# The int8 feed-forward part taken by halves of 512 rows, with its down products regrouped

## The chip, the cores and the metric

The kernel runs on one core of one Trainium2 chip. The metric is the device time of one execution in microseconds (us); the kernel before has a median of 733.33 us over three runs (732.94 to 734.95). TensorE (PE) multiplies, VectorE (DVE), ScalarE (ACT) and GpSimd (POOL) work on rows of 128 partitions, SyncE (SP) and ScalarE start the transfers (DMA) that matter here. The program gives each engine its instructions in one fixed order.

## The reference, cut to what matters

Two transformer layers over a (4, 256, 256) input. The last part is a feed-forward layer with int8 weights, added to its input and layer-normed. As called here, `x` has 1,024 rows of 256; the hidden width is 1,024.

```python
def _qmatmul(x, w_int8, scale):
    y = jnp.einsum('bsh,ho->bso', x, w_int8.astype(x.dtype))
    return y * scale
gate = silu(_qmatmul(x, w_gate, s_gate))
up = _qmatmul(x, w_up, s_up)
x = _layernorm(x + _qmatmul(gate * up, w_down, s_down))
```

What comes ahead of it (rotary attention with 16 heads, a feed-forward layer with a Hadamard transform, an mLSTM block with its own feed-forward layer) takes the first 675 us and is computed in the same way in both kernels.

## The kernel before, in words

The int8 values are kept as `F32R`, a 32-bit type whose products the trace shows as one matmul record each; an activation is split into a high part in that type and the rest (`rest`, L856), so every product is the sum of two. The part works batch by batch, 256 rows each:

- `ffn2_in` (L868) transposes a batch's rows (four 128x128 transposes, L876, into one PSUM bank), takes the high part with a ScalarE copy (L878) and the low part with a DVE subtraction (L857): tile `qx`.
- `ffn2_up` (L882) makes, for each of `NH` = 8 blocks of 128 hidden columns, the gate and the up product side by side in one PSUM bank, 256 columns each: four matmuls each, two chunks of the contraction times high and low part (`mm_parts`, L861). Then come SiLU on ScalarE (L890), scaling and product on DVE (L891), the high part on ScalarE (L894), the low part on DVE for odd blocks and on GpSimd for even ones (L857): tile `qh`.
- `ffn2_sums` (L901) makes the down products: for each of a batch's two tiles of 128 rows, 16 matmuls of 256 columns (L909) into a bank `po`. DVE scales them, adds the input and takes mean and variance (L914, L915, L502, L503).
- `ffn2_down` (L918) computes the inverse root on DVE alone, by a bit trick and three Newton steps (`rsqrt`, L50 to L63: 13 small instructions), normalizes on DVE (L924) and writes the batch out. The last batch, `ffn2_end` (L932), takes the root from ScalarE (L939) and one Newton step on DVE instead, normalizes one row tile on each engine and writes by two queues. ScalarE loads the table for the root (L898) at the end of the last up block.

The banks come from two cycles: `bank("d")` hands out `mm` and `sc` in turn, `bank("m")` `pt` and `ot`; each name has two buffers, so four banks are in turn on either side. The order is written by hand at the end: up products of batch 0, with those of batch 2 begun in between, then batch 1 and 3; a batch's down products stand some blocks after its last up block. A scheduler then orders the instructions of each engine by this.

Just ahead stands the second half's `ffn1` (rows 512 to 1,023 of the layer before): 32 fp32 down products (L561), and a layernorm of its last rows on DVE with the same 13-instruction root (L53 to L63, L512), which gives `xb[1]`.

Of the kernel before, what the change touches and what calls it, by code (L numbers as in the profile page):

```python
# [24 lines left out]
NH = FF // P  # L25
HALF = NT // 2
NJH = HALF // P
# [3 lines left out]
LN_EPS = 1e-5  # L31
# [7 lines left out]
def tile_two_layers(ctx: ExitStack, tc: tile.TileContext, a: dict, out: bass.AP):  # L39
    nc = tc.nc  # L40

    const = ctx.enter_context(tc.tile_pool(name="const", bufs=1))
    small = ctx.enter_context(tc.tile_pool(name="small", bufs=3))
    psum = ctx.enter_context(tc.tile_pool(name="psum", bufs=2, space=bass.MemoryType.PSUM))

    def bank(tag):
        return psum.tile([P, 512], F32, tag=tag, name=f"ps_{tag}")


    def rsqrt(v, n, scale, eps):  # L50

        ve = small.tile([P, n], F32, tag="rs_v", name="rs_v")
        nc.vector.tensor_scalar(ve, v, scale, eps, ALU.mult, ALU.add)  # L53
        sh = small.tile([P, n], I32, tag="rs_sh", name="rs_sh")
        nc.vector.tensor_single_scalar(sh, ve.bitcast(I32), 1, ALU.logical_shift_right)
        y = small.tile([P, n], F32, tag="rs_y", name="rs_y")
        nc.vector.tensor_scalar(y.bitcast(I32), sh, -1.0, RSQRT_MAGIC, ALU.mult, ALU.add)
        nc.vector.tensor_scalar_mul(ve, ve, -0.5)
        t = small.tile([P, n], F32, tag="rs_t", name="rs_t")
        for _ in range(3):  # L60
            nc.vector.tensor_tensor(t, y, y, ALU.mult)
            nc.vector.tensor_tensor(t, t, ve, ALU.mult)
            nc.vector.scalar_tensor_tensor(y, t, 1.5, y, ALU.add, ALU.mult)  # L63
        return y
# [14 lines left out]
    ps = bank("pt")  # L79
# [45 lines left out]
    ident = cst[:, 896:1024]  # L125
# [276 lines left out]
    ps = {}  # L402
    prs = {}
    rest = []
    for bb in range(2):
# [3 lines left out]
        po = bank("ot")  # L409
# [29 lines left out]
    rest = []  # L439
    for bb in range(2):  # L440
        po = bank("ot")
# [9 lines left out]
    work = ctx.enter_context(tc.tile_pool(name="work", bufs=2))  # L451
# [38 lines left out]
    xb = [work.tile([P, NJH, D], F32, tag=f"xb{n}", name=f"xb{n}", bufs=1) for n in halves]  # L490
    xs = [work.tile([P, NJH, D], F32, tag=f"xs{n}", name=f"xs{n}", bufs=1) for n in halves]
# [112 lines left out]
    bias = mix.tile([2 * 32, 2], F32, tag="bias", name="bias")  # L604
# [251 lines left out]
    def rest(engine, v, hi, lo):  # L856
        engine.tensor_tensor(lo, v, hi.bitcast(F32), ALU.subtract)  # L857
# [5 lines left out]
    out_v = out.rearrange("b (t p) d -> p b t d", p=P)  # L863

    def rows_of(t, b):
        return t[b // 2][:, 2 * (b % 2) : 2 * (b % 2) + 2, :]

    def ffn2_in(b):  # L868

        xd = rows_of(xb, b)  # L870
        x = work.tile([P, 2, KC, S], F32R, tag="fm", name="qx")
        pt = bank("d")
        for c in range(KC):
            for j in range(2):
                at = c * S + j * P
                nc.tensor.transpose(pt[:, at : at + P], xd[:, j, c * P : (c + 1) * P], ident)  # L876
        by_c = pt.rearrange("p (c s) -> p c s", c=KC)
        nc.scalar.copy(x[:, 0], by_c)  # L878
        rest(nc.vector, by_c, x[:, 0], x[:, 1])
        return x  # L880

    def ffn2_up(x, hT, last=False):  # L882
        for c in range(NH):
            cols = slice(c * P, (c + 1) * P)
            ps = bank("d")
            pg, pu = ps[:, 0:S], ps[:, S:]
            for dst, w in ((pg, q_gate), (pu, q_up)):
                mm_parts(dst, [(w[:, i, cols], x[:, k, i, :]) for i in range(KC) for k in range(2)])
            g = split.tile([P, S], F32, tag="gq", name="gq", bufs=4)
            nc.scalar.activation(g, pg, AF.Silu, scale=s_gu[:, c : c + 1])  # L890
            nc.vector.scalar_tensor_tensor(  # L891
                g, pu, s_gu[:, NH + c : NH + c + 1], g, ALU.mult, ALU.mult
            )
            copied = nc.scalar.copy(hT[:, 0, c, :], g)  # L894
            rest(nc.vector if c % 2 else nc.gpsimd, g, hT[:, 0, c, :], hT[:, 1, c, :])
            if last and c == NH - 1:
                with tc.issue_after(copied.ins):
                    nc.scalar.activation(small.tile([P, 1], F32, tag="junk1", name="junk1"), eps, AF.Sqrt)  # L898
            yield 0.9

    def ffn2_sums(b, hT, mv):  # L901


        xd, xe = rows_of(xb, b), rows_of(xs, b)
        po = [bank("m")[:, :D] for _ in range(2)]
        for j, blocks in ((0, range(0, NH - 1)), (1, range(0, NH // 2)), (0, (NH - 1,)), (1, range(NH // 2, NH))):
            for i in blocks:
                for k in range(2):
                    nc.tensor.matmul(  # L909
                        po[j], lhsT=hT[:, k, i, j * P : (j + 1) * P], rhs=q_down[:, i, :],  # L910
                        start=(i == 0 and k == 0), stop=(i == NH - 1 and k == 1),
                    )
        for j in range(2):
            nc.vector.tensor_tensor(xe[:, j, :], po[j], s_down, ALU.mult)  # L914
            nc.vector.tensor_tensor(xe[:, j, :], xe[:, j, :], xd[:, j, :], ALU.add)  # L915
            statistics(xe[:, j, :], mv[:, j, :])

    def ffn2_down(b, hT):  # L918
        xe = rows_of(xs, b)
        mv = small.tile([P, 2, 2], F32, tag="out_mv", name="out_mv")  # L920
        ffn2_sums(b, hT, mv)
        rstd = rsqrt(mv[:, :, 1], 2, 1.0, LN_EPS)
        for j in range(2):
            nc.vector.tensor_scalar(  # L924
                xe[:, j, :], xe[:, j, :], mv[:, j, 0:1], rstd[:, j : j + 1], ALU.subtract, ALU.mult
            )
        nc.sync.dma_start(out_v[:, b], xe)

    eps = late.tile([P, 1], F32, tag="eps", name="eps")
    nc.gpsimd.memset(eps, LN_EPS)  # L930

    def ffn2_end(b, hT):  # L932


        xe = rows_of(xs, b)
        mv = small.tile([P, 2, 2], F32, tag="out_mv", name="out_mv")
        ffn2_sums(b, hT, mv)
        root = small.tile([P, 2], F32, tag="rs_v", name="root")
        nc.scalar.activation(root, mv[:, :, 1], AF.Sqrt, bias=eps)  # L939
        ve = small.tile([P, 2], F32, tag="rs_sh", name="ve")  # L940
        nc.vector.tensor_scalar(ve, mv[:, :, 1], LN_EPS, -0.5, ALU.add, ALU.mult)
        rstd = small.tile([P, 2], F32, tag="rs_y", name="rstd")
        nc.vector.reciprocal(rstd, root)
        t = small.tile([P, 2], F32, tag="rs_t", name="rs_t")
        nc.vector.tensor_tensor(t, rstd, rstd, ALU.mult)
        nc.vector.tensor_tensor(t, t, ve, ALU.mult)
        nc.vector.scalar_tensor_tensor(rstd, t, 1.5, rstd, ALU.add, ALU.mult)
        shift = small.tile([P, 1], F32, tag="shift", name="shift")
        nc.vector.scalar_tensor_tensor(shift, mv[:, 0, 0:1], -1.0, rstd[:, 0:1], ALU.mult, ALU.mult)
        nc.vector.tensor_scalar(  # L950
            xe[:, 1, :], xe[:, 1, :], mv[:, 1, 0:1], rstd[:, 1:2], ALU.subtract, ALU.mult
        )
        nc.sync.dma_start(out_v[:, b, 1:2], xe[:, 1:2])
        nc.scalar.activation(xe[:, 0, :], xe[:, 0, :], AF.Identity, bias=shift, scale=rstd[:, 0:1])
        nc.scalar.dma_start(out_v[:, b, 0:1], xe[:, 0:1])


    def merge(first, other):
# [26 lines left out]
    one = ffn1(0, "d")  # L985
# [4 lines left out]
    left = one  # L990
    merge(mlstm(1), left)
    mix.release()
    split = tc.alloc_tile_pool(name="split", bufs=3, side="right")
    qh = [split.tile([P, 2, NH, S], F32R, tag="qh", name=f"qh{b}") for b in range(3)]
    one = ffn1(1, "m")
    merge(chain(take(1, one), [6.0]), left)
    run(left)
    run(one)
    ups, hts = {}, qh

    def begin(b):
        ups[b] = ffn2_up(ffn2_in(b), hts[b], b == B - 1)

    begin(0)
    run(take(5, ups[0]))
    begin(2)
    run(ups[0])
    run(take(2, ups[2]))
    begin(1)
    run(take(2, ups[2]))  # L1010
    ffn2_down(0, hts[0])
    run(ups[2])
    hts.append(split.tile([P, 2, NH, S], F32R, tag="qh", name="qh3"))
    begin(3)
    run(take(4, ups[1]))
    ffn2_down(2, hts[2])
    run(ups[1])
    run(take(4, ups[3]))
    ffn2_down(1, hts[1])
    run(ups[3])  # L1020
    ffn2_end(3, hts[3])
    split.release()
    hid.release()
    wts.release()


# [93 lines left out]
```

## Time and profile before

| what | before |
|---|---|
| median of 3 runs | 733.33 us (732.94 to 734.95) |
| the profiled execution | 733.4 us, of which its span on the core is 731.6 us |
| PE busy | 719.2 us, 98% of the span |
| DVE, ACT, POOL busy | 406.8, 242.2, 179.6 us |
| first int8 up product | 675.71 us |
| last batch's down products begin | 720.09 us |
| last transfer is issued | 728.57 us |
| granted TensorE clock | 0.998 of full |

The profile comes from one execution. Times in the trace are counted from the span's start. A matmul's duration in the trace includes its way through the array, and neighbours overlap; what a matmul costs in a stream is therefore the distance from one start to the next. An fp32 product stands in the trace as two matmul records.

### The profile page before, as it was taken

Reading aid. Unit: us, or ns where it says so; the run is one execution under the profiler, and the core shown is the slowest. Engines: PE = TensorE matmul, PEld = TensorE weight load, DVE = VectorE, ACT = ScalarE, POOL = GpSimd, SP = SyncE. Lnnn points to the kernel's source line nnn. Section 1 sums busy time; section 2 is a strip of 40 time slices with the busy share of each in tenths; the row PEclk is TensorE's granted clock in tenths of the full one; section 3 lists DMA queues with packets and bytes.
Section 4 is the critical chain, followed back from the end, with each engine's and each line's share of the span. In section 5 each row is a group of like instructions: output and inputs, shape, how many; then the busy total and the mean of one; then the engine's idle time right before and its main releaser. Section 6 shows DMA issues by size and latency. Waiting matters only on the chain.

```text
span 731.6 us, 8898 instructions
## 1 busy us (share of the span) xinstructions
PE 719.2 (98%) x3084; PEld 491.0 (67%) x3084; DVE 406.8 (56%) x1063; ACT 242.2 (33%) x651; POOL 179.6 (25%) x197
## 2 busy tenths in 40 slices
PE   8999999999999999999999999999999999999996
PEld 4657667667767766766776864745775476747995
DVE  0363545555564364455445464374778458844797
ACT  2232432342242243233224331126411461111563
POOL 1721431449441242144044000002200050000221
PEclk9999999999999999999999999999999999999999
DMA  7542143173223222421311322002030110000001
GB/s 233 226 115 55 21 113 59 31 272 58 39 91 58 52 86 52 93 59 37 72 37 22 58 70 56 1 0 87 31 115 1 56 61 1 0 1 0 2 16 43
DMA packets 48108, 45.36 MB, mean 62 GB/s; under 512 B 9504, under 2 KB 42688, under 8 KB 46016
## 3 DMA queue, kind: packets, MB, share of 16 engines
q1 hardware_dynamic: 46928, 40.47, 21.1%
q0 software_dynamic: 432, 3.15, 1.2%
q10 hardware_dynamic: 704, 1.18, 0.5%
q8 instruction: 24, 0.39, 0.3%
q14 instruction: 20, 0.16, 0.1%
HBM read 25.61 MB, written 1.08 MB: 36 GB/s over the span
## 4 chain that ended last, share of the span: by engine, by line
PE 88%; DVE 6%; DMA 2%; ACT 1%; issue 1%; POOL 0%; DVEq 0%; SPq 0%; ACTq 0%; POOLq 0%
PE ps_mm L69 37%; PE ps_d L69 11%; PE ps_ot L69 8%; PE ps_m L69 6%; PE ps_d L561 5%; PE ps_pt L232 4%; PE ps_sc L232 4%; PE ps_sc L241 2%; PE ps_d L861 2%; PE ps_m L561 2%; PE ps_m L778 2%; PE ps_pt L241 2%; DMA wide<-far 1%; PE ps_m L909 1%; DVE gq L891 1%; DMA w_qkv<-in_w_qkv 1%
## 5 line engine op out<-in xcount | busy, mean ns | idle before, releaser
L69 PE MATMUL ps_mm<-xT,w_qkv 128*128 128x512 f32 x248 | 115.7, 593 | 0.0
L176 POOL TENSOR_TENSOR rope_raw<-rope_raw,cst 128x512 f32<-128x512 f32 x32 | 40.7, 1271 | 229.8 <-DVE rope_swp L173 229.8
L260 ACT ACTIVATE pr<-ps_sc,nmax 128x256 f32<-128x256 f32 x64 | 29.5, 472 | 142.2 <-DVE nmax L251 142.2
L69 PEld LDWEIGHTS ps_mm<-xT,w_qkv 128*128 128x128 f32 x248 | 47.0, 190 | 37.2 <-issue 33.8
L69 PEld LDWEIGHTS ps_ot<-prT,v 128*128 128x128 f32 x240 | 45.6, 190 | 28.8 <-issue 25.3
L69 PE MATMUL ps_ot<-prT,v 128*128 128x256 f32 x240 | 60.8, 379 | 0.0
L69 PE MATMUL ps_mm<-w_o,oT 128*128 128x256 f32 x256 | 60.6, 380 | 0.0
L270 DVE TENSOR_SCALAR pr<-pr,rinv 128x256 f32<-128x256 f32 x128 | 58.1, 487 | 1.8
L69 PE MATMUL ps_mm<-xT,w_rot 128*128 128x512 f32 x128 | 59.0, 604 | 0.0
L69 PE MATMUL ps_mm<-w_qkv,xT 128*128 128x256 f32 x256 | 58.1, 379 | 0.6 <-ACT kn L198 0.6
L69 PEld LDWEIGHTS ps_mm<-w_o,oT 128*128 128x128 f32 x256 | 48.4, 190 | 12.9 <-issue 6.0
L69 PE MATMUL ps_d<-fm,w 128*128 128x512 f32 x128 | 56.7, 594 | 0.3 <-ACT fm L538 0.3
L69 PEld LDWEIGHTS ps_mm<-w_qkv,xT 128*128 128x128 f32 x256 | 48.6, 190 | 8.4 <-ACT kn L198 1.0
L251 DVE TENSOR_REDUCE nmax<-ps_sc 128x2 f32<-128x512 f32 x32 | 20.6, 686 | 59.1 <-PE ps_sc L241 59.1
L756 POOL TENSOR_TENSOR ex<-cst,wide 128x512 f32<-128x512 f32 x16 | 19.9, 1265 | 131.8 <-DMA wide<-far 119.4
L210 DVE COPY v<-ps_mm 128x512 f32<-128x512 f32 x32 | 22.0, 691 | 50.4 <-PE ps_mm L69 46.8
L268 DVE RECIPROCAL rinv<-rsum 128x2 f32<-128x2 f32 x64 | 9.7, 152 | 64.3 <-ACT pr L260 64.1
L278 DVE STREAM_TRANSPOSE cross<-pr 128x512 f32<-128x512 f32 x60 | 42.7, 711 | 1.5
L69 PEld LDWEIGHTS ps_d<-fm,w 128*128 128x128 f32 x128 | 24.0, 190 | 27.1 <-issue 24.9
L69 PEld LDWEIGHTS ps_mm<-xT,w_rot 128*128 128x128 f32 x128 | 23.2, 189 | 28.1 <-issue 20.4
L177 POOL TENSOR_TENSOR rope_swp<-rope_swp,cst 128x512 f32<-128x512 f32 x32 | 40.8, 1274 | 0.0
L857 POOL TENSOR_TENSOR qh<-gq,qh 128x256 fp32r<-128x256 f32 x16 | 12.3, 766 | 108.8 <-issue 79.6
(199 smaller groups left out, 1227.5 us busy)
## 6 DMA issues: line engine op xcount, KB each, us to landing
prT<-cross SPq DMA_DIRECT2D x240, 64.0 KB, 2.1
w_qkv<-in_w_qkv SPq DMA_DIRECT2D x7, 1024.0 KB, 5.2
wide<-far SPq DMA_DIRECT2D x8, 512.0 KB, 4.0
w<-in_w SPq DMA_DIRECT2D x3, 1024.0 KB, 13.7
w_o<-in_w_o SPq DMA_DIRECT2D x8, 256.0 KB, 3.1
acc<-in_x SPq DMA_DIRECT2D x2, 512.0 KB
w_gate<-in_w_gate SPq DMA_DIRECT2D x1, 1024.0 KB, 8.7
w_up<-in_w_up SPq DMA_DIRECT2D x1, 1024.0 KB, 10.6
```

Source lines behind the costliest of these rows:

```text
L69: nc.tensor.matmul(ps, lhsT=lhs(i), rhs=rhs(i), start=(i == 0), stop=(i == n - 1))
L176: nc.gpsimd.tensor_tensor(by_b(raw), by_b(raw), cs, ALU.mult)
L177: nc.gpsimd.tensor_tensor(by_b(swp), by_b(swp), sn, ALU.mult)
L210: return nc.vector.tensor_copy(v[:, 2 * jj : 2 * jj + 2, :], ps.rearrange("p (t d) -> p t d", t=2))
L232: nc.tensor.matmul(ps[bb][e][:, qt * S : (qt + 1) * S], lhsT=qn[:, e, queries(bb, qt)], rhs=kn[:, e, keys(bb)], start=(qt == 0), stop=Fals ...
L241: nc.tensor.matmul(ps[bb][e][:, qt * S : (qt + 1) * S], lhsT=qr[rows, queries(bb, qt)], rhs=kr[rows, keys(bb)], start=False, stop=(qt == 1 ...
L251: nc.vector.tensor_reduce(nmax, ps.rearrange("p (t k) -> p t k", t=2), AX.X, ALU.max, negate=True)
L260: nc.scalar.activation(pr[:, qt, :], ps[:, qt * S : (qt + 1) * S], AF.Exp, bias=nmax[:, qt : qt + 1], accum_out=rsum[:, qt : qt + 1],)
L270: nc.vector.tensor_scalar(pr[:, qt, :], pr[:, qt, :], rinv[:, qt : qt + 1], None, ALU.mult)
L278: return nc.vector.transpose(cross[:, :, e], pr.rearrange("p t (x i) -> p x t i", i=32))
L561: nc.tensor.matmul(po, lhsT=hT[:, i, j * P : (j + 1) * P], rhs=wd[:, i, :], start=(i == 0), stop=(i == NH - 1))
L756: nc.gpsimd.tensor_tensor(ex, mask.unsqueeze(1).to_broadcast([P, 4, P]), wide[:, 2 * k : 2 * k + 2, :].rearrange("p h (c s) -> p (h c) s", ...
```

## The change

The int8 part works on halves of two batches, 512 rows, instead of single batches.

- `ffn2_in(n)` makes eight transposes for a half, into two banks, with two ScalarE copies and two DVE subtractions of 512 columns. The first half's stand among the last down products of `ffn1`.
- `ffn2_up` uses one bank for the gate product and one for the up product, each of 512 columns; all that follows works on 512 columns. There are 16 blocks instead of 32. In the last half, the low parts of blocks 4 to 7 are all made on DVE.
- The down products of batch 0 stand after four blocks of the second half; those of batches 1, 2 and 3 follow each other after the last up block.
- All four batches take the root from ScalarE (`root_rsqrt`), behind the load of its table, and normalize one row tile on each engine. Batches 0 to 2 are written in one transfer each, batch 3 in two.
- The second half's `qh` lies in a pool of its own, in the place of the tiles that `ffn1` used.

```diff
-        x = work.tile([P, 2, KC, S], F32R, tag="fm", name="qx")
-        pt = bank("d")
+        x = split.tile([P, 2, KC, HALF], F32R, tag="qx", name="qx")
         for c in range(KC):
-            for j in range(2):
-                at = c * S + j * P
-                nc.tensor.transpose(pt[:, at : at + P], xd[:, j, c * P : (c + 1) * P], ident)
-        nc.scalar.copy(x[:, 0], by_c)
-        rest(nc.vector, by_c, x[:, 0], x[:, 1])
+            pt = bank("d")
+            for j in range(NJH):
+                nc.tensor.transpose(
+                    pt[:, j * P : (j + 1) * P], xb[n][:, j, c * P : (c + 1) * P], ident
+                )
+            nc.scalar.copy(x[:, 0, c], pt)
+            rest(nc.vector, pt, x[:, 0, c], x[:, 1, c])
...
-            ps = bank("d")
-            pg, pu = ps[:, 0:S], ps[:, S:]
+            pg, pu = bank("d"), bank("d")
...
-            rest(nc.vector if c % 2 else nc.gpsimd, g, hT[:, 0, c, :], hT[:, 1, c, :])
+            rest(nc.vector if c % 2 or last and c >= NH // 2 else nc.gpsimd, g, hT[:, 0, c, :], hT[:, 1, c, :])
...
+    def root_rsqrt(v):
+
+        root = small.tile([P, 2], F32, tag="rs_v", name="root")
+        with tc.issue_after(rooted[0].ins):
+            nc.scalar.activation(root, v, AF.Sqrt, bias=eps)
+        ve = small.tile([P, 2], F32, tag="rs_sh", name="ve")
+        nc.vector.tensor_scalar(ve, v, LN_EPS, -0.5, ALU.add, ALU.mult)
+        y = small.tile([P, 2], F32, tag="rs_y", name="rstd")
+        nc.vector.reciprocal(y, root)
+        t = small.tile([P, 2], F32, tag="rs_t", name="rs_t")
+        nc.vector.tensor_tensor(t, y, y, ALU.mult)
+        nc.vector.tensor_tensor(t, t, ve, ALU.mult)
+        nc.vector.scalar_tensor_tensor(y, t, 1.5, y, ALU.add, ALU.mult)
+        return y
...
-    begin(0)
-    run(take(5, ups[0]))
-    begin(2)
-    run(ups[0])
-    run(take(2, ups[2]))
-    begin(1)
-    run(take(2, ups[2]))
-    ffn2_down(0, hts[0])
-    run(ups[2])
-    hts.append(split.tile([P, 2, NH, S], F32R, tag="qh", name="qh3"))
-    begin(3)
-    run(take(4, ups[1]))
-    ffn2_down(2, hts[2])
-    run(ups[1])
-    run(take(4, ups[3]))
-    ffn2_down(1, hts[1])
-    run(ups[3])
-    ffn2_end(3, hts[3])
+    run(take(1 + 2 * NH + 2 * NJH - 3, one))
+    x = ffn2_in(0)
+    run(one)
+    hid.release()
+    end = tc.alloc_tile_pool(name="end", bufs=1)
+    hts.append(end.tile([P, 2, NH, HALF], F32R, tag="qh1", name="qh1"))
+    first = ffn2_up(x, hts[0])
+    run(take(3, first))
+    x = ffn2_in(1)
+    run(first)
+    second = ffn2_up(x, hts[1], last=True)
+    run(take(4, second))
+    po = ffn2_sums(0, hts[0])
+    run(second)
+    ffn2_down(0, po)
+    for b in range(1, B):
+        ffn2_down(b, ffn2_sums(b, hts[b // 2]), b == B - 1)
```

More of the change, by code (lines that the diff above doesn't have):

```diff
@@ L866, in rows_of, with ffn2_in @@
         return t[b // 2][:, 2 * (b % 2) : 2 * (b % 2) + 2, :]
-    def ffn2_in(b):
-        xd = rows_of(xb, b)
-        x = work.tile([P, 2, KC, S], F32R, tag="fm", name="qx")
-        pt = bank("d")
+    def ffn2_in(n):
+        x = split.tile([P, 2, KC, HALF], F32R, tag="qx", name="qx")
         for c in range(KC):
-            for j in range(2):
-                at = c * S + j * P
-                nc.tensor.transpose(pt[:, at : at + P], xd[:, j, c * P : (c + 1) * P], ident)
-        by_c = pt.rearrange("p (c s) -> p c s", c=KC)
-        nc.scalar.copy(x[:, 0], by_c)
-        rest(nc.vector, by_c, x[:, 0], x[:, 1])
+            pt = bank("d")
[5 more added lines that the diff above has]
+            rest(nc.vector, pt, x[:, 0, c], x[:, 1, c])
         return x
+    rooted = []
     def ffn2_up(x, hT, last=False):
@@ L884, in ffn2_up @@
             cols = slice(c * P, (c + 1) * P)
-            ps = bank("d")
-            pg, pu = ps[:, 0:S], ps[:, S:]
+            pg, pu = bank("d"), bank("d")
             for dst, w in ((pg, q_gate), (pu, q_up)):
                 mm_parts(dst, [(w[:, i, cols], x[:, k, i, :]) for i in range(KC) for k in range(2)])
-            g = split.tile([P, S], F32, tag="gq", name="gq", bufs=4)
+            g = split.tile([P, HALF], F32, tag="gq", name="gq", bufs=4)
             nc.scalar.activation(g, pg, AF.Silu, scale=s_gu[:, c : c + 1])
@@ L894, in ffn2_up, with ffn2_sums @@
             copied = nc.scalar.copy(hT[:, 0, c, :], g)
-            rest(nc.vector if c % 2 else nc.gpsimd, g, hT[:, 0, c, :], hT[:, 1, c, :])
+            rest(nc.vector if c % 2 or last and c >= NH // 2 else nc.gpsimd, g, hT[:, 0, c, :], hT[:, 1, c, :])
             if last and c == NH - 1:
                 with tc.issue_after(copied.ins):
[L898 to L904, printed above, removed]
+                    rooted.append(
+                        nc.scalar.activation(small.tile([P, 1], F32, tag="junk1", name="junk1"), eps, AF.Sqrt)
+                    )
+            yield 1.8
+    def ffn2_sums(b, hT):
         po = [bank("m")[:, :D] for _ in range(2)]
+        at = b % 2 * S
         for j, blocks in ((0, range(0, NH - 1)), (1, range(0, NH // 2)), (0, (NH - 1,)), (1, range(NH // 2, NH))):
@@ L909, in ffn2_sums, with ffn2_rows @@
                     nc.tensor.matmul(
-                        po[j], lhsT=hT[:, k, i, j * P : (j + 1) * P], rhs=q_down[:, i, :],
+                        po[j], lhsT=hT[:, k, i, at + j * P : at + (j + 1) * P], rhs=q_down[:, i, :],
                         start=(i == 0 and k == 0), stop=(i == NH - 1 and k == 1),
                     )
+        return po
+    def ffn2_rows(b, po):
+        xd, xe = rows_of(xb, b), rows_of(xs, b)
+        mv = small.tile([P, 2, 2], F32, tag="out_mv", name="out_mv", bufs=3)
         for j in range(2):
@@ L916, in ffn2_sums @@
             statistics(xe[:, j, :], mv[:, j, :])
[L918 to L927, printed above, removed]
+        return xe, mv
@@ L929, in tile_two_layers @@
     eps = late.tile([P, 1], F32, tag="eps", name="eps")
     nc.gpsimd.memset(eps, LN_EPS)
[L932 to L937, printed above, removed]
+    def root_rsqrt(v):
         root = small.tile([P, 2], F32, tag="rs_v", name="root")
-        nc.scalar.activation(root, mv[:, :, 1], AF.Sqrt, bias=eps)
+        with tc.issue_after(rooted[0].ins):
+            nc.scalar.activation(root, v, AF.Sqrt, bias=eps)
@@ L940, in ffn2_end @@
         ve = small.tile([P, 2], F32, tag="rs_sh", name="ve")
-        nc.vector.tensor_scalar(ve, mv[:, :, 1], LN_EPS, -0.5, ALU.add, ALU.mult)
-        rstd = small.tile([P, 2], F32, tag="rs_y", name="rstd")
-        nc.vector.reciprocal(rstd, root)
+        nc.vector.tensor_scalar(ve, v, LN_EPS, -0.5, ALU.add, ALU.mult)
+        y = small.tile([P, 2], F32, tag="rs_y", name="rstd")
+        nc.vector.reciprocal(y, root)
         t = small.tile([P, 2], F32, tag="rs_t", name="rs_t")
-        nc.vector.tensor_tensor(t, rstd, rstd, ALU.mult)
+        nc.vector.tensor_tensor(t, y, y, ALU.mult)
@@ L946, in ffn2_end, with ffn2_down @@
         nc.vector.tensor_tensor(t, t, ve, ALU.mult)
-        nc.vector.scalar_tensor_tensor(rstd, t, 1.5, rstd, ALU.add, ALU.mult)
+        nc.vector.scalar_tensor_tensor(y, t, 1.5, y, ALU.add, ALU.mult)
+        return y
+    def ffn2_down(b, po, end=False):
+        xe, mv = ffn2_rows(b, po)
+        rstd = root_rsqrt(mv[:, :, 1])
         shift = small.tile([P, 1], F32, tag="shift", name="shift")
         nc.vector.scalar_tensor_tensor(shift, mv[:, 0, 0:1], -1.0, rstd[:, 0:1], ALU.mult, ALU.mult)
-        nc.vector.tensor_scalar(
-            xe[:, 1, :], xe[:, 1, :], mv[:, 1, 0:1], rstd[:, 1:2], ALU.subtract, ALU.mult
-        )
@@ L953, in ffn2_end @@
-        nc.sync.dma_start(out_v[:, b, 1:2], xe[:, 1:2])
-        nc.scalar.activation(xe[:, 0, :], xe[:, 0, :], AF.Identity, bias=shift, scale=rstd[:, 0:1])
-        nc.scalar.dma_start(out_v[:, b, 0:1], xe[:, 0:1])
+        for j in (1, 0):
+            if not j:
+                nc.scalar.activation(xe[:, j, :], xe[:, j, :], AF.Identity, bias=shift, scale=rstd[:, j : j + 1])
+            else:
+                nc.vector.tensor_scalar(
+                    xe[:, j, :], xe[:, j, :], mv[:, j, 0:1], rstd[:, j : j + 1], ALU.subtract, ALU.mult
+                )
+            if end:
+                (nc.sync if j else nc.scalar).dma_start(out_v[:, b, j : j + 1], xe[:, j : j + 1])
@@ L958, in merge @@
+        if not end:
+            nc.sync.dma_start(out_v[:, b], xe)
     def merge(first, other):
@@ L992, in tile_two_layers @@
     mix.release()
-    split = tc.alloc_tile_pool(name="split", bufs=3, side="right")
-    qh = [split.tile([P, 2, NH, S], F32R, tag="qh", name=f"qh{b}") for b in range(3)]
+    split = tc.alloc_tile_pool(name="split", bufs=2, side="right")
+    hts = [split.tile([P, 2, NH, HALF], F32R, tag="qh", name="qh0", bufs=1)]
     one = ffn1(1, "m")
@@ L997, in tile_two_layers @@
     run(left)
+    run(take(1 + 2 * NH + 2 * NJH - 3, one))
+    x = ffn2_in(0)
     run(one)
-    ups, hts = {}, qh
-    def begin(b):
-        ups[b] = ffn2_up(ffn2_in(b), hts[b], b == B - 1)
-    begin(0)
-    run(take(5, ups[0]))
-    begin(2)
-    run(ups[0])
-    run(take(2, ups[2]))
-    begin(1)
-    run(take(2, ups[2]))
-    ffn2_down(0, hts[0])
-    run(ups[2])
-    hts.append(split.tile([P, 2, NH, S], F32R, tag="qh", name="qh3"))
-    begin(3)
-    run(take(4, ups[1]))
-    ffn2_down(2, hts[2])
-    run(ups[1])
-    run(take(4, ups[3]))
-    ffn2_down(1, hts[1])
-    run(ups[3])
-    ffn2_end(3, hts[3])
+    hid.release()
[12 more added lines that the diff above has]
+        ffn2_down(b, ffn2_sums(b, hts[b // 2]), b == B - 1)
+    end.release()
     split.release()
-    hid.release()
     wts.release()
```

## The prediction, made before the changed kernel ran

> **What bounds the kernel now.** I read the page's first part (busy time by engine), then the busy time by stage, the groups of the last stage with shapes apart, the chain that ended last, and the timeline of the end. In the stage table the columns are the stretch, its length, the busy time of PE, PEld, DVE, ACT and POOL, the clock, and the DMA share and rate:
>
> ```profile
> PE 719.2 (98%) x3084; PEld 491.0 (67%) x3084; DVE 406.8 (56%) x1063; ACT 242.2 (33%) x651; POOL 179.6 (25%) x197
> ...
> 634.50:675.70 41.20, 41.20 (x129) 24.25 (x129) 21.71 (x63) 6.64 (x10) 0.00 (x0) 1.00 0.00 1
> 675.70:720.10 44.40, 43.78 (x367) 43.31 (x366) 38.41 (x123) 25.67 (x64) 11.53 (x15) 1.00 0.04 13
> 720.10:731.60 11.50, 4.25 (x34) 3.84 (x32) 7.49 (x31) 3.74 (x8) 0.73 (x1) 0.85 0.14 46
> ```
>
> Up to 720.1 the int8 part is TensorE's, nearly without a gap; only the last 11.5 us are DVE's. The second thing to see is PEld: with 512 columns moving (634.5 to 675.7 is mostly that) the weight loads fill 59% of the time, with 256 columns 98%. The chain (start, us, what) gives the price of a record in each shape, its time divided by its count:
>
> ```profile
> 634.54 27.70 PE ps_m L69 x64
> 662.25 13.83 PE ps_m L561 x64
> ...
> 682.09 5.02 PE ps_d L861 x40
> ...
> 701.28 2.89 PE ps_m L909 x24
> ```
>
> fp32 records: 433 ns at 512 columns, 216 ns at 256; both 0.845 ns a column. `F32R` records at 256 columns (L861, L909): 120 to 125 ns here with their waits; the undisturbed stretch 704.95 to 712.46 has 64 in 7.51 us, 117.4 ns. Half the fp32 price would be 108. So a 256-column record costs 9 ns more than its columns.
>
> The end, after the last up product (start, us, engine, line):
>
> ```profile
> 720.09 1.73 PE L909 MATMUL ps_m<-q_down,qh 128*128 128x256 f32 x13
> 722.15 2.54 PE L909 MATMUL ps_m<-q_down,qh 128*128 128x256 f32 x19 [0.34 <-POOL qh L857]
> 722.17 1.28 ACT L898 ACT_TABLE_LOAD   x1
> 723.79 0.42 DVE L914 TENSOR_TENSOR xs<-ps_m,s_down 128x256 f32<-128x256 f32 x1
> 726.63 0.29 ACT L939 ACTIVATE root<-out_mv,eps 128x2 f32<-128x2 f32 x1 [2.96 <-DVE out_mv L503]
> 728.57 0.37 ACTq L955 DMA_DIRECT2D out<-xs  x1
> ```
>
> **What the Trainium skill says.** "TensorE: Matmul & The Clock Gate", section Back-to-back issue gap: a warm matmul takes N / 2.4 + 2.5 ns, so 109 ns for 256 columns and 216 for 512; its section LDWEIGHTS gives columns / 1.2, 107 ns for 128. The trace has 117.4 where both are nearly equal, and PEld full: I read the extra 9 ns as the weight load, no longer covered. No `F32R` record of 512 columns is in this trace. "VectorE: DVE Perf Modes", section The DRAIN you can't avoid, has every operation wait for the pipe to empty; the trace is milder: a dependent 256-column operation follows after 0.46 us, an independent one after 0.34, a small one is fitted in for 0.07. "ScalarE: Activation LUTs", section What ACT_TABLE_LOAD costs: 1,283 ns plus a drain of 1,380; the trace has the 1.28 us, and the next activation 0.02 us behind it, so no such drain.
>
> **The change, part by part.** The instruction orders of both programs, engine by engine, are the same up to the first transposes of the int8 part.
>
> Up products. 256 records by 117.4 ns, 30.05 us, become 128 of 512 columns. Price of one: the best witness is the fp32 record of 256 columns, which occupies the array as long as 512 `F32R` columns should and has a weight load of its own: 216.1 to 216.5 ns. Below this I see no reason (512 columns by 0.4225 are 216). Above: 225.6 if the 9 ns come with every record; 235 if price only follows columns. I take 216.4: 27.70 us, a gain of 2.35.
>
> Transposes: 16 at 0.11 us (four in 0.44) before and after. Four move ahead of the first up product: it starts 0.44 later, at 676.15; eight remain behind it, 0.88 instead of 12, 1.32. Sum nothing. The first four, early at 634, take only rows whose layernorm is over (row tiles 0 and 1); the rest stand after 20 of 32 down products, when `xb[0]` is long complete (640.6 plus 1.15 at the latest). Their copies and subtractions (2 x 0.58 on ScalarE, 2 x 0.68 on DVE) end near 674, ahead of 676.15; the SiLU table's load, 1.28, fits as well.
>
> Waits of TensorE. Before, 720.09 - 675.71 = 44.38 us hold 30.05 of up products, 11.49 of three batches' down products (32 at 119.7 ns, 3.83 each) and 1.32 of transposes; 1.52 are waits, around 680 and 682: DVE reaches the first L891 only behind `ffn1`'s last layernorm. After: that chain starts 0.44 later and frees DVE at 679.94; L891 at 512 columns takes 0.69 (L553's row), so the first bank comes free at 680.69, needed at 680.47: 0.22. The transposes of the second half want `xb[1]` (681.6) and the second block's bank (682.3): 0.16 more. Then the two 0.58 copies, queued on ScalarE among high-part copies, delay the fourth SiLU and DVE's subtractions, and the bank of the fifth up product by 0.1; refilling costs 0.1 three times less what overlaps. I take 0.65. From then a block has 1.73 us of TensorE, against 1.2 on ScalarE (SiLU 0.60, copy 0.58) and at most 1.38 on DVE: covered. A bank must be free 2.59 us after its up product ended; SiLU and L891 need 0.9.
>
> Down products in the middle: 3.83, unchanged, all inputs long there.
>
> So the close begins at 676.15 + 27.70 + 0.88 + 3.83 + 0.65 = 709.21.
>
> The close. TensorE needs 3 x 3.83 = 11.49 us, without waits (`qh` of both halves is complete 2.5 us in, batch 2 starts at 3.83). DVE follows in order. Times from the close's start: last L891 ends about 1.2 (its SiLU stands behind two copies), copy to 1.8, DVE's low part to 2.5; table load to 3.1, dummy 3.3, batch 0's root to 3.65. Batch 1's first rows come at 3.06 (24 of 32 products and 0.19 of latency, as at 689.29 to 692.35). DVE then has, for each batch, L922, L923, statistics twice, six small ones, one normalization; two batches' instructions alternate. By the distances above, from one batch's first L922 to the next's: 0.34 + 0.12 + 0.34 + 0.08 + 0.34 + 0.34 + 0.32 + 0.12 + 0.46 + 0.46, then 0.55 to the reciprocal (root on ScalarE in between) and 0.2 + 0.2 + 0.08, 3.95. TensorE gives a batch each 3.83, so DVE paces, by little. Batch 1 takes 4.30, since it begins with 0.3 us of waiting for the table and batch 0's root stands in it: L922 of batch 2 at 7.36, of batch 3 at 11.30. From there to the last issue: before, 728.57 - 723.79 = 4.78; plus 0.3 for the three instructions of batch 2 in it; and 3.03 to the end of the span, as before. The close takes 11.30 + 8.11 = 19.41. Before, from 720.09: 11.51 with one batch's products. Without products 7.92 against 7.68: 0.24 lost, though the 0.34 wait for GpSimd's low part is gone.
>
> Roots: three of 13 small DVE instructions become six; in the old middle they lay beside TensorE, worth nothing there. Without this the close would pay seven more at 0.2 per batch, 4 us. The three batch outputs (256 KB, 2.2 us to landing) go on SP's queue with nothing behind but the last batch's, 3 us later. GpSimd has six low parts of 1.27 us (L176's row), each within two blocks.
>
> Sum: -2.35 (up products) - 0.87 (waits) + 0.24 (close) = -2.98. Span 728.6; the profiled execution 733.4 - 3.0 = 730.4; on the median 733.33, which is 0.07 lower, **730.3 us**.
>
> **The rivals.** (1) A 512-column `F32R` record isn't cheaper than two halves: at 225.6 ns the gain shrinks by 1.18 (731.5), at 235 by 2.38 (732.7). For it: no such record in the trace. Against it: fp32's proportional prices, and the full PEld. (2) Two blocks in the banks instead of four: DVE's or ScalarE's lateness at the start lasts into more blocks. If each of the first half's last five blocks waits 0.3 us, 731.8. For it: DVE is over 90% busy from 700 to 720 before. Against it: its work falls to 1.38 of 1.73. (3) Slower: the close turns into a relay of DVE and ScalarE. Batch b's normalization on ScalarE (L953, 0.60) stands before batch b+1's root; if that waits for it, DVE stands still at the reciprocal with everything of the next batch behind it. Slower by 0.3% needs 5.2 us more, 1.7 in each of three batches, a period of 5.7 instead of 3.95. It decides from where L953 ends later than the next statistics; by my times it ends near 6.3, and those at 6.5, so small slips cost tenths, not 1.7. That gives 735.5 and more.
>
> **How the numbers follow.** 0.3% is 2.2 us, about what a measurement of this kernel can tell from no change. Forecast (729.2 to 731.1): 0.72. Rival 1: 0.12, nearly all within 0.3%. Rival 2: 0.09, within. Rival 3: 0.07. Faster 0.73, same 0.20, slower 0.07. The range goes from 729.2 (DVE keeps to TensorE in the close, fewer waits) to 732.2, which takes in rival 1's fixed 9 ns and rival 2, and leaves out its proportional case and rival 3.
>
> **What would show it.** Right: L861 records 216 to 217 ns apart and PEld well below full; TensorE idle 0.5 to 1 us between 680 and 687 and nowhere else until the close; close at 709.2, batch 3's first L922 11.3 later, the last issue 16.4 later. Wrong: records 225 ns apart or more; gaps ahead of L861 in every block; long waits of the reciprocal for the root.

## The result, and the profile after

The changed kernel takes 730.76 us (median of seven runs, 730.62 to 732.93); seven runs of the kernel before beside it have a median of 734.57 us. The ratio is 0.9965, with a 95% interval of 0.9953 to 0.9977: faster by 0.35%, just above what can be told from no change. One thing has to be known to read the times: executions of one kernel fall into two groups some 2 us apart, and of the twelve profiles of this case five have 3.67 us for the first eight matmuls (L185; before is one of them) and seven have 5.64 to 6.08 us (after is one of them, with 732.8 us and a span of 731.0), which fits the two groups though no run tested it; between executions of the like group the two kernels differ by 2.0 to 2.2 us.

So the two traces are compared from a point behind this: the start of `ffn1`'s glu products in the second half (L69), up to the issue of the last transfer. Before that is 634.54 to 728.57, 94.03 us. After it is 636.12 to 727.98, 91.86 us. **The gain is 2.17 us**, where 2.98 had been predicted.

First the page's busy time by engine for the kernel after:

```profile
PE 719.4 (98%) x2956; PEld 485.1 (66%) x2956; DVE 398.8 (55%) x1017; ACT 238.8 (33%) x625; POOL 175.1 (24%) x187
```

The sums hardly differ from those of before; the count of matmuls is down by 128. Then its busy time by stage (stretch, length, PE, PEld, DVE, ACT, POOL, clock, DMA share and rate). The first stretch is the part of the up products between the second half's transposes and the first down products, the second the close:

```profile
684.20:700.70 16.50, 16.50 (x76) 13.64 (x75) 10.77 (x16) 11.22 (x21) 5.34 (x5) 1.00 0.00 0
709.50:731.00 21.50, 13.96 (x107) 13.33 (x105) 14.95 (x56) 7.83 (x15) 0.00 (x0) 0.91 0.15 49
```

In the up stage TensorE has no gap, the weight loads fill 83% of it instead of 98%, and DVE is down to 65%. So far it is as the prediction had it. Now the chain that ended last (start, us, what), cut to the pieces that answer to those of before:

```profile
636.12 27.70 PE ps_m L69 x64
...
678.07 5.52 PE ps_d L861 x24
683.60 0.87 PE ps_d L874 x8
684.47 16.37 PE ps_d L861 x72
700.84 3.83 PE ps_m L911 x32
```

72 up records in 16.37 us are 227 ns each. The timeline of TensorE shows it without any sum; the two lines are neighbouring groups of four (start, us, line and tiles):

```profile
696.14 1.07 PE L861 MATMUL ps_d<-qx,q_up 128*128 128x512 f32 x4
697.05 1.07 PE L861 MATMUL ps_d<-qx,q_gate 128*128 128x512 f32 x4
```

From one group's start to the next it is 0.907 us over a longer stretch, **226.7 ns a record**. The 128 records, 32 groups, take 29.0 us where 27.70 were predicted and where before's 256 took 30.05. The forecast gain of 2.35 was 1.05.

Last the close, which begins at 711.79. From the timelines of TensorE, DVE and ScalarE; the three L922 are the first rows of batches 1, 2 and 3:

```profile
711.79 11.67 PE L911 MATMUL ps_m<-q_down,qh 128*128 128x256 f32 x96
...
714.87 0.42 DVE L922 TENSOR_TENSOR xs<-ps_m,s_down 128x256 f32<-128x256 f32 x1 [0.44 <-PE ps_m L911]
718.98 0.42 DVE L922 TENSOR_TENSOR xs<-ps_m,s_down 128x256 f32<-128x256 f32 x1
722.88 0.42 DVE L922 TENSOR_TENSOR xs<-ps_m,s_down 128x256 f32<-128x256 f32 x1
726.37 0.17 DVE L938 RECIPROCAL rstd<-root 128x2 f32<-128x2 f32 x1 [0.22 <-ACT root L934]
727.98 0.37 ACTq L959 DMA_DIRECT2D out<-xs  x1
```

Counted from 711.79, the batches' first rows are taken at 3.08, 7.19 and 11.09 and the last transfer is issued at 16.19; the prediction had 3.06, 7.36, 11.30 and 16.4. The bracket on the reciprocal is its wait for ScalarE's root: 0.22 us, and three such waits make 0.5 us in all.

### The profile page after: what moved, and what is told of

It reads as the page before. It is cut to its first block, busy times and chain, and to the rows that moved or that the text cites. A ratio compares the mean times of both kernels' runs of the same rounds, so it can differ in the third digit from the quotient of the medians.

```text
span 731.0 us, 8563 instructions
## 1 busy us (share of the span) xinstructions
PE 719.4 (98%) x2956; PEld 485.1 (66%) x2956; DVE 398.8 (55%) x1017; ACT 238.8 (33%) x625; POOL 175.1 (24%) x187
## 4 chain that ended last, share of the span: by engine, by line
PE 91%; DVE 4%; ACT 2%; DMA 1%; issue 1%; POOL 0%; DVEq 0%; ACTq 0%
PE ps_mm L69 37%; PE ps_d L69 11%; PE ps_ot L69 8%; PE ps_m L69 8%; PE ps_d L561 5%; PE ps_pt L232 4%; PE ps_sc L232 4%; PE ps_d L861 4%; PE ps_sc L241 2%; PE ps_m L561 2%; PE ps_m L778 2%; PE ps_pt L241 2%; PE ps_mm L185 1%; DMA w_qkv<-in_w_qkv 1%; PE ps_m L534 1%; ACT ex L763 1%
## 5 line engine op out<-in xcount | busy, mean ns | idle before, releaser
L69 PE MATMUL ps_mm<-xT,w_qkv 128*128 128x512 f32 x248 | 115.8, 593 | 0.0
L69 PEld LDWEIGHTS ps_mm<-xT,w_qkv 128*128 128x128 f32 x248 | 47.0, 190 | 37.2 <-issue 33.8
L69 PEld LDWEIGHTS ps_ot<-prT,v 128*128 128x128 f32 x240 | 45.6, 190 | 28.8 <-issue 25.4
L69 PE MATMUL ps_ot<-prT,v 128*128 128x256 f32 x240 | 60.8, 379 | 0.0
L69 PE MATMUL ps_mm<-w_o,oT 128*128 128x256 f32 x256 | 60.6, 380 | 0.0
L69 PE MATMUL ps_mm<-xT,w_rot 128*128 128x512 f32 x128 | 59.0, 604 | 0.0
L69 PE MATMUL ps_mm<-w_qkv,xT 128*128 128x256 f32 x256 | 58.1, 379 | 0.3 <-ACT kn L198 0.3
L69 PE MATMUL ps_d<-fm,w 128*128 128x512 f32 x128 | 56.7, 594 | 0.3 <-ACT fm L538 0.3
L69 PEld LDWEIGHTS ps_mm<-w_o,oT 128*128 128x128 f32 x256 | 48.4, 190 | 12.9 <-issue 6.0
L69 PEld LDWEIGHTS ps_mm<-w_qkv,xT 128*128 128x128 f32 x256 | 48.6, 190 | 8.1 <-issue 1.0
L69 PEld LDWEIGHTS ps_d<-fm,w 128*128 128x128 f32 x128 | 24.0, 190 | 27.1 <-issue 24.9
L69 PEld LDWEIGHTS ps_mm<-xT,w_rot 128*128 128x128 f32 x128 | 23.2, 189 | 28.1 <-issue 20.4
L552 ACT ACTIVATE glu_g<-ps_d 128x512 f32<-128x512 f32 x24 | 14.2, 592 | 67.4 <-PE ps_d L69 67.4
```

The source lines that it names most:

```text
L69: nc.tensor.matmul(ps, lhsT=lhs(i), rhs=rhs(i), start=(i == 0), stop=(i == n - 1))
```

## The experiments

Each starts from the changed kernel. Beside the median and its ratio to the kernel before stands the time from the common point (the start of L69) to the issue of the last transfer in the profiled execution, 91.86 us for the kernel after. Differences from the kernel after are read from this time, since the medians of a run were taken beside those of the kernel before and not of the kernel after. Where only one execution of a kernel was made, its total time tells little, and distances inside its trace are used.

### What a moving column costs

**Two times 256 columns.** Everything of the change stays, but each up product is again made of records of 256 columns.

```diff
-                mm_parts(dst, [(w[:, i, cols], x[:, k, i, :]) for i in range(KC) for k in range(2)])
+                for lo, hi in ((0, 256), (256, 512)):
+                    mm_parts(dst[:, lo:hi], [(w[:, i, cols], x[:, k, i, lo:hi]) for i in range(KC) for k in range(2)])
```

> The changed kernel, with every up product of 512 columns made as two of 256, all else the same. Theory A (an F32R record costs some 8 to 10 ns beside its columns, whatever its size): a 256-column record is again 117 ns apart from the next, the 32 groups of the part last 30.05 instead of 29.0 us, and the kernel is about 1.0 us slower than the changed one (it would be 731.8 where that has 730.8). Rival B (the price follows the columns, and what 256 columns pay more is only the weight load): with the granted 227 ns for 512 columns, 256 would cost 113 ns by their columns but are held at 117 by weight loads, which must then fill PEld; the same 1.0 us, so this run alone only gives the worth of the columns; the 384-column run tells A from B.

733.52 us, ratio 0.9993 [0.9982, 1.0003]; 635.94 to 729.54, 93.60 us, 1.74 more than the kernel after. Its busy time in the up stage (columns as above), where the weight loads fill all of it:

```profile
684.30:701.50 17.20, 17.20 (x146) 17.20 (x144) 10.54 (x16) 11.03 (x20) 5.17 (x4) 1.00 0.00 1
```

And its groups of eight records on TensorE's timeline:

```profile
686.27 1.12 PE L861 MATMUL ps_d<-qx,q_gate 128*128 128x256 f32 x8
687.23 1.12 PE L861 MATMUL ps_d<-qx,q_up 128*128 128x256 f32 x8
```

Eight records in 0.96 us are 120.0 ns each, and 120 is the distance from each record to the next all through the stretch. With 512 columns the record is worth 1.7 us here: without it, what is left of the gain is 0.43 us (94.03 against 93.60), and the median cannot be told from before. Against before itself, whose 256-column records cost 117.4 ns, it is worth the 1.05 us above. The direction was expected, the size not: the price expected was 117 ns, as in the kernel before. Why before's 256 columns cost 2.6 ns less than these stays open.

The two prices also part the record into two terms: 226.7 - 120.0 = 106.7 ns for 256 further columns, 0.417 ns a column, and so 13 ns that every record pays, if the price is a straight line between the two. Four runs ask what the 13 ns are.

**Weights in another order.** The two parts of the activation that share a weight chunk no longer follow each other, so that no record has the weights of the one ahead of it.

```diff
-                mm_parts(dst, [(w[:, i, cols], x[:, k, i, :]) for i in range(KC) for k in range(2)])
+                mm_parts(dst, [(w[:, i, cols], x[:, k, i, :]) for k in range(2) for i in range(KC)])
```

> The changed kernel, with the four matmuls of each product in another order: the weights alternate from one to the next, where the high and low part with the same weights stood side by side. If the fixed part of a record comes from the weights being changed (and loading the same again is cheaper), records go from 226.7 to 229 ns or more, as the down products, which change weights every time, cost 119.6 against 117.4 for the kernel before's up products. If the fixed part is the record's own: 226.7 again, the span within 0.3 us.

One execution: 733.01 us; 636.30 to 728.17, 91.87 us. TensorE's timeline:

```profile
690.00 1.07 PE L861 MATMUL ps_d<-qx,q_gate 128*128 128x512 f32 x4
690.90 1.07 PE L861 MATMUL ps_d<-qx,q_up 128*128 128x512 f32 x4
```

Four records again take 0.907 us. The order of the weights does nothing.

**384 and 128 columns.** The split of the first experiment with `((0, 384), (384, 512))`.

> The changed kernel, with every up product of 512 columns made as one of 384 and one of 128. The distances from record to record so far: 226.7 ns at 512 columns in the changed kernel, 119.9 at 256 in the run with 256 columns, else the same. Theory A (columns at one per 2.4 GHz cycle, 0.4167 ns, and a fixed 13 ns per record): 173 ns at 384. Rival B (the price goes with the columns, 0.443 ns each, and 256 columns are held up by the weight load alone): 170 ns at 384. Both: 128 columns show the floor of a weight load; if that is below 115 ns, the weight load isn't what 256 columns wait for. The span grows by 128 times (384 and 128 together less 226.7), some 7 us if 128 columns cost 108.

One execution: 741.3 us, and from the common point 100.2 us, 8.3 more than the kernel after, where some 7 were expected. Groups of eight, four of 384 and four of 128 columns (the line names the first shape), follow each other at 1.15 us in TensorE's timeline:

```profile
693.47 1.32 PE L861 MATMUL ps_d<-qx,q_gate 128*128 128x384 f32 x8
694.62 1.32 PE L861 MATMUL ps_d<-qx,q_up 128*128 128x384 f32 x8
```

Inside the first of them the starts are 693.70, 693.88, 694.06 and 694.23 for its later wide records and the first narrow one, so 384 columns cost 177 ns; 173 are expected with fixed 13 ns, 170 in proportion. Both are missed by more than they differ, and the wide records alone don't decide. The narrow ones follow each other at 0.110 to 0.112 us, which is near what the Trainium skill has for a weight load of 128 columns ("TensorE: Matmul & The Clock Gate", section LDWEIGHTS: 107 ns); only the second one starts 0.06 us after the first, and its load had time while the wide records ran. These 60 ns lie between the 66 of a fixed 13 ns and the 57 of a price in proportion, so they don't decide either. What the run shows is the floor that was asked for: four records in a row with a load each take 110 to 112 ns, and a record of 256 columns at 120.0 isn't held up by the rate of the loads.

**Each product twice.** Every up product is made twice into its bank; the second sum begins anew, so the result is the first one's. DVE, ScalarE and GpSimd then have twice the time for a block.

```diff
-                mm_parts(dst, [(w[:, i, cols], x[:, k, i, :]) for i in range(KC) for k in range(2)])
+                for _ in range(2):
+                    mm_parts(dst, [(w[:, i, cols], x[:, k, i, :]) for i in range(KC) for k in range(2)])
```

> The changed kernel, with the four matmuls of each up product made twice (the second time they begin the sum anew), so that TensorE does double work while DVE, ScalarE and GpSimd do the same as before and are busy half as much. If the fixed part is the record's own: 226.7 ns again, the span 128 times that, 29.0 us, longer (less the 0.3 us of waits near 680). Rival: the other engines' reads and writes slow TensorE's; then records come nearer 216 ns, and the span grows by 27 to 28 us.

One execution: 759.35 us; 633.83 to 754.53, 120.70 us, 28.84 more. Busy time in a stretch of 8 us of this kernel (columns as above):

```profile
690.00:698.00 8.00, 8.00 (x37) 6.64 (x36) 2.19 (x3) 2.77 (x5) 1.30 (x1) 1.00 0.00 0
```

In the same stretch of the kernel after, DVE is busy for 5.02 us, ScalarE for 5.17 and GpSimd for 2.91, about twice as much; TensorE makes the same 37 records in it. In its timeline eight take 1.813 us, 226.6 ns each. So the 13 ns are neither a hidden wait for a bank nor traffic of the other engines.

**bf16 in place of `F32R`.** Weights of the up products and both parts of the activation are kept as bf16. Int8 weights are exact in it; the activation's two parts together keep some 16 bits. (The definition of the type and a change to `rest` that lets it read a bf16 high part are left out here.)

```diff
-        x = split.tile([P, 2, KC, HALF], F32R, tag="qx", name="qx")
+        x = split.tile([P, 2, KC, HALF], BF16, tag="qx", name="qx")
...
-    q_gate, q_up, q_down = (ff_weight(k, nc.gpsimd, F32R) for k in ("q_gate", "q_up", "q_down"))
+    q_gate, q_up = (ff_weight(k, nc.gpsimd, BF16) for k in ("q_gate", "q_up"))
+    q_down = ff_weight("q_down", nc.gpsimd, F32R)
```

> The changed kernel, with the weights and both parts of the activations of the gate and up products held in bf16 instead of F32R (the int8 weights are exact in it, the activation's two parts keep some 16 bits); the down products stay in F32R. In the program a bf16 product is a weight load and a matmul, an F32R product one instruction that does both. Theory: the fixed 13 ns belong to the F32R form; a bf16 record of 512 columns then costs 216 ns, what the prediction took, and the part is 128 x 10.7 ns, 1.4 us, faster than the changed kernel. Rival: the 13 ns come with the 512 columns themselves (their reads, or the write of a whole bank); then 227 again and no gain.

730.70 us, ratio 0.9957 [0.9941, 0.9973]; 635.83 to 726.38, 90.55 us, 1.31 less than the kernel after. TensorE's timeline (the edit moves this part down by one line, so L862 is the L861 of the others):

```profile
690.74 1.03 PE L862 MATMUL ps_d<-qx,q_gate 128*128 128x512 bf16 x4
691.60 1.03 PE L862 MATMUL ps_d<-qx,q_up 128*128 128x512 bf16 x4
```

16 groups take 13.81 us, 215.8 ns a record; 128 records by 10.9 ns less are 1.40 us, of which 1.31 arrive. The fixed cost goes with the form `F32R`: bf16 has 2.5 ns of it, as a formula of the Trainium skill has it ("TensorE: Matmul & The Clock Gate", section Back-to-back issue gap: columns / 2.4 + 2.5 for a warm matmul; the section calls it the gap of a single matmul and gives about 131 ns for 512 columns in a stream, which the 215.8 here contradict).

What it is in that form stays open, for the edit changes the load of the weights along with the rest. Three groups of weight loads (count, busy time, mean ns of one), the first from before's fp32 down products, the second from the kernel after, the third from the last run below, in bf16:

```profile
L561 PEld LDWEIGHTS ps_m<-w_down,hT 128*128 128x128 f32 x64 | 12.2, 190 | 2.1 <-issue 0.5
L861 PEld LDWEIGHTS ps_d<-qx,q_gate 128*128 128x128 f32 x64 | 11.9, 188 | 2.4
L862 PEld LDWEIGHTS <-q_gate 128*128 128x128 bf16 x63 | 6.2, 98 | 6.8
```

A load record lasts half as long in bf16. Its length alone isn't the cause: the fp32 records have a load of 190 ns each and follow at 216 ns. In the program an `F32R` product is one instruction that loads and multiplies, a bf16 product has a load of its own; that the 13 ns lie in this is only argued, and a rival, the four bytes of each moving element against two, was not tested.

### The close and the moved work

**Roots of batches 0 to 2 on DVE again**, by the 13 small instructions; batch 3 keeps ScalarE's root.

```diff
-        rstd = root_rsqrt(mv[:, :, 1])
+        rstd = root_rsqrt(mv[:, :, 1]) if end else rsqrt(mv[:, :, 1], 2, 1.0, LN_EPS)
```

> The changed kernel, with the roots of batches 0 to 2 made by the 13 small DVE instructions again; batch 3 keeps the root on ScalarE. What the prediction said of this edit: seven more small ones at 0.2 us in each of three batches, 4 us on the close. Theory now, from the distances in the trace of the changed kernel: batch 0's root fits beside the last blocks and costs nothing; batches 1 and 2 pay eight dependent steps of 0.2 instead of the 0.95 us over ScalarE and five more fitted in at 0.07, 1.0 each; the close takes 21.2 instead of 19.2 us, the kernel 2 us more. Rival: DVE has slack in the close and nothing changes (below 0.3 us).

731.23 us, ratio 0.9968 [0.9956, 0.9981]; 634.65 to 726.57, 91.92 us, 0.06 more than the kernel after. The theory of 2 us fell. The timelines of DVE and ScalarE, with the close beginning at 710.33:

```profile
713.40 0.42 DVE L922 TENSOR_TENSOR xs<-ps_m,s_down 128x256 f32<-128x256 f32 x1 [0.16 <-PE ps_m L911]
...
717.25 0.16 DVE L63 SCALAR_TENSOR_TENSOR rs_y<-rs_t,rs_y 128x2 f32<-128x2 f32 x1
717.44 0.16 DVE L61 TENSOR_TENSOR rs_t<-rs_y 128x2 f32<-128x2 f32 x1
717.52 0.42 DVE L922 TENSOR_TENSOR xs<-ps_m,s_down 128x256 f32<-128x256 f32 x1
717.85 0.15 DVE L62 TENSOR_TENSOR rs_t<-rs_t,rs_v 128x2 f32<-128x2 f32 x1
717.97 0.42 DVE L923 TENSOR_TENSOR xs<-xs,xb 128x256 f32<-128x256 f32 x1
...
721.58 0.42 DVE L922 TENSOR_TENSOR xs<-ps_m,s_down 128x256 f32<-128x256 f32 x1
726.57 0.37 ACTq L959 DMA_DIRECT2D out<-xs  x1
```

The batches' first rows stand at 3.07, 7.19 and 11.25 from the close's start, against 3.08, 7.19 and 11.09. Seven more instructions a batch cost next to nothing. The trace shows three things that make up for them; how they share in it is not worked out. Those that stand behind the next batch's first large instruction run in the pauses after the large ones and take 0.07 to 0.12 us (L62 at 717.85, L923 at 717.97). Those ahead of it still take 0.2 each (717.25, 717.44), but there DVE of the kernel after waits for ScalarE's root, 0.2 us in each batch. And batch 0's root is made by the close's start and no longer stands inside batch 1 behind the load of the table.

**Low parts of blocks 4 and 6 of the last half on GpSimd**, as in the other halves.

```diff
-            rest(nc.vector if c % 2 or last and c >= NH // 2 else nc.gpsimd, g, ...
+            rest(nc.vector if c % 2 else nc.gpsimd, g, ...
```

> The changed kernel, with the low parts of the last half's blocks 4 and 6 on GpSimd again, as in all other even blocks. Theory: nothing (within 0.3 us): the last SiLU, which leads to the table load and the first root, stands behind two copies on ScalarE and not behind DVE, and batch 2 asks for these parts 3.8 us after the last up block. Rival: the last blocks' low parts come late from GpSimd (1.3 us each) and TensorE waits in the close, 0.5 to 1.5 us more.

732.12 us, ratio 0.9972 [0.9962, 0.9983]; 635.93 to 727.75, 91.82 us: no difference. GpSimd's last low part ends at 712.81, 1.24 us into the close (from 711.57); but the close begins with batch 1, from the first half, and the products that read it come only 3.83 us in.

**Two batches' down products in the middle.** Those of batch 1 go behind block 6 of the last half, so that two batches are left for the close.

```diff
-    run(second)
+    run(take(2, second))
+    po1 = ffn2_sums(1, hts[0])
+    run(second)
     ffn2_down(0, po)
-    for b in range(1, B):
+    ffn2_down(1, po1)
+    for b in range(2, B):
```

> The changed kernel, with batch 1's down products moved from the close to behind block 6 of the second half, so that only two batches are left. Theory: DVE paces the close at 3.9 us a batch against TensorE's 3.83, and falls behind by 0.3 us in its first batch while the table is loaded; with two batches the last one's first scaling is nearer TensorE's time: 0.3 to 0.5 us faster. Rival: batch 0's and batch 1's roots now both wait for the table and are crowded into the first batch of the close: 0.3 to 1 us slower.

732.02 us, ratio 0.9968 [0.9955, 0.9981]; 634.26 to 726.01, 91.75 us, 0.11 less than the kernel after, and less than expected. That is little above the 0.06 us by which the runs without an effect differ from it; having batch 1's rows out of DVE's way in the close is worth a tenth of a microsecond at most. What is left is seen in DVE's timeline: the last batch's row tiles are taken at 720.88 and 721.75, both at the end, since the order of the products ends with blocks of either; from the second to the last issue it is 4.26 us.

**The same, with the last batch row tile by row tile.** Batch 3's first row tile gets all its 16 products before the second one has any.

```diff
-        for j, blocks in ((0, range(0, NH - 1)), (1, range(0, NH // 2)), (0, (NH - 1,)), (1, range(NH // 2, NH))):
+        for j, blocks in ((0, range(0, NH)), (1, range(0, NH))) if b == B - 1 else ...:   # the old order
```

> The kernel with batch 1's down products in the middle (0.1 us better than the changed one from a common point in the trace), and the last batch's down products made for one row tile and then for the other, instead of interleaved. Theory: the first tile's sums are there 1.9 us ahead of the second's and not 0.96, DVE has scaled, added and taken the statistics of it when the second comes, and the chain behind the last product shrinks: 0.3 to 0.6 us faster than the changed kernel. Rival: DVE is still at the batch before and only takes what it can: within 0.2 us.

732.10 us, ratio 0.9968 [0.9956, 0.9980]; 635.76 to 727.16, 91.40 us, 0.46 less than the kernel after, as expected. TensorE and DVE at the end:

```profile
715.28 7.86 PE L911 MATMUL ps_m<-q_down,qh 128*128 128x256 f32 x64
723.30 0.42 DVE L922 TENSOR_TENSOR xs<-ps_m,s_down 128x256 f32<-128x256 f32 x1
727.16 0.37 ACTq L959 DMA_DIRECT2D out<-xs  x1
```

DVE takes the last row tile 0.16 us after TensorE's last product ended (715.28 + 7.86), and the last transfer goes out 3.86 us after that, 0.40 less than in the run before: that tail of sums, statistics and normalization is left.

**Both together: the last order, and all int8 products in bf16.** The down products' weights and `qh` become bf16 as well.

> The order of the run with two batches in the middle and the last batch by row tiles, and every product of the int8 part in bf16. Theory: 1.4 us from the up products, and the down products from 119.6 to 109 ns a record, 128 times, 1.4 us, of which in the close only what DVE lets through; with the 0.5 us of the order 2.5 to 3 us faster than the changed kernel. Rival: 256 columns stay near 117 to 120, since there the weight load is the bound: 1.9 us.

729.37 us, ratio 0.9947 [0.9928, 0.9966]; 634.14 to 723.59, 89.45 us, 2.41 less than the kernel after and just short of the 2.5 to 3 expected. By this time it is the fastest of all the kernels here; its activations keep some 16 bits here too. TensorE and the last transfer:

```profile
697.69 3.66 PE L912 MATMUL ps_m<-q_down,qh 128*128 128x256 bf16 x32
701.18 1.03 PE L862 MATMUL ps_d<-qx,q_gate 128*128 128x512 bf16 x4
723.59 0.37 ACTq L960 DMA_DIRECT2D out<-xs  x1
```

32 down products of 256 columns take 3.49 us to the next group's start, 109.1 ns each instead of 119.7. Two batches of them in the middle save 0.68 us; with 1.31 from the up products and 0.46 from the order that is 2.45, and 2.41 came. At 256 columns bf16 thus saves 10.6 ns a record, at 512 it saved 10.9: the excess of `F32R` hardly depends on the width, which is the better witness for a fixed cost than the straight line through two widths.

## Why the prediction was right, and where it was wrong

The time is in the range and close to the forecast, but closer than the mechanism earned, by luck: the medians of this comparison are 3.8 us apart, the traces from the common point 2.17. Of the 2.98 predicted 0.8 is missing, and one term, the price of a record, was mis-sized by more than that.

- **Up products: the price of a 512-column `F32R` record.** The step "the best witness is the fp32 record of 256 columns" put it at 216.4 ns; it is 226.7. The gain is 1.05 instead of 2.35 us, 1.3 less. The step before it failed with it: "I read the extra 9 ns as the weight load, no longer covered". The loads were without a pause by the profile (PEld 98%), and yet their rate was not the cause: the narrow records show that loads can follow each other at 110 ns, not 117 to 120, and with 512 columns the extra cost is still there while PEld is at 83%. The 59% that the prediction took for wide records is a mean: fp32 records of 512 columns have 44% (640 to 660 us), those of 256 have 88% (663 to 675 us), and these have no excess. It is a fixed cost of the `F32R` record that the fp32 record does not have, so the witness was of another kind. The prediction's first rival, with 225.6 ns, is what happened; it said 731.5.
- **Transposes**: 0.44 us ahead of the first up product. From the start of L69 to the first up product it was 41.17 before and is 41.60. Right.
- **Waits of TensorE**: 0.65 predicted. From the first up product (677.72) to the close (711.79) there are 34.07 us; 29.0 of up products, 0.87 of transposes and 3.83 of down products leave 0.37. The size is better by 0.3, but the waits that were forecast did not occur. Before has two for a bank, 0.6 us in all; the first stands here, and under it what answers to it in the kernel after:

```profile
680.17 0.75 PE L861 MATMUL ps_d<-qx,q_gate 128*128 128x256 f32 x4 [0.36 <-DVE gq L891]
681.52 0.75 DVE L891 SCALAR_TENSOR_TENSOR gq<-ps_d,s_gu,gq 128x512 f32<-128x512 f32 x1
682.50 1.10 PE L861 MATMUL ps_d<-qx,q_up 128*128 128x512 f32 x4
```

L891 ends at 682.27, just when the prediction had it (680.69, and 1.58 for the later common point), but the sixth up product comes to its bank only at 682.50. Twenty records stand ahead of it, and at 226.7 ns they take 0.2 us longer than at 216.4: that is where the forecast wait of 0.22 went. The profile lists no wait of TensorE from 672 to 712. About 0.19 of the 0.37 is the first record's start, which is stamped 0.03 us after that of the last `ffn1` record, though that one takes 0.216; the rest is in records a few ns longer than the others. The second rival did not occur.

- **Down products in the middle**: 3.83. Right.
- **The close**: 16.4 to the last issue predicted, 16.19 measured; every mark within 0.21. Right, and DVE paces by as little as was said. The third rival, a relay of DVE and ScalarE, did not occur: the waits for the root are 0.2 us, not 1.7.
- **Roots**: "Without this the close would pay seven more at 0.2 per batch, 4 us" was wrong. It shows 0.06. The prediction's own figure for a small one fitted in, 0.07, was the one to use for a part of them, and from the saving DVE's wait for ScalarE was not taken off.

Against the forecast the terms are 1.3 us worse (up products), 0.3 better (waits) and 0.2 better (close): 0.8 together, the difference of 2.98 and 2.17. The first two are not independent, since the dearer records swallowed a forecast wait. The 2.17 us themselves are, rounding aside, 1.05 from the records and 1.15 from waits (1.52 before, 0.37 after), less 0.05 in the close (to the last issue and without the 7.66 of two batches' products 8.53, against 8.48 before): the records, which were to bring most of the gain, brought less than half of it.

## What to carry to other kernels

Price a matmul of a type and width by a record of the same type, and where only one width is in the trace, keep open that its excess over the columns is fixed per record; a busy weight load beside it does not prove that it is the cause. To find which part of a change pays, undo one part and read the distance between two fixed points of the trace: here it agreed within 0.06 us for kernels whose change had no effect, where the runs' own spread is 2. Small dependent instructions cost their full distance only when nothing else stands in the queue; where two independent chains alternate, taking some of them away can give nothing.

## What the runs showed of the hardware

- A record of `F32R` took 226.7 ns with 512 columns and 120.0 with 256 (117.4 in the kernel before); bf16 records of the same shapes took 215.8 and 109.1. The line through the first two is 0.417 ns a column and 13 ns. In a stream bf16 is 5% faster at 512 columns and 9% at 256.
- fp32 records of 256 columns follow at 216 ns with a weight load of 190 ns each, so a long load record alone brings no excess. A load record of `F32R` lasts 188 ns, one of bf16 98.
- Records of `F32R` with 128 columns and a weight load each follow at 110 to 112 ns, and the loads overlap the records ahead (one pair stands 60 ns apart, where the load had time before).
- Neither the order of the weights nor twice the time for the other engines changed the record by more than 0.2 ns.
